# A decoder layer on one core: attention recorded as six streams instead of four, and a group prepared in two pairs of sequences

## The chip, the core and the metric

The kernel runs on one NeuronCore of a Trainium2 chip. The metric is the device time of one execution in microseconds. TensorE is called PE, its weight loads PEld, VectorE is DVE, ScalarE is ACT, GpSimd is POOL, and SyncE, which issues most DMAs, is SP. All data are 32-bit floats.

## What is computed

The reference is one pre-norm decoder layer over 32 sequences of 100 tokens with 256 features, and a context of 361 rows for each sequence:

```python
x = x + self_attention(layernorm(x))            # 16 heads of 16, rotary positions, causal
x = x + cross_attention(layernorm(x), ctx)      # 16 heads of 16, 361 keys, with biases
x = x + soft_moe(layernorm(x))                  # 8 experts of 128 slots

def soft_moe(x):
    xn, sn = rmsnorm(x), rmsnorm(slot_embeds)
    logits = einsum('bnd,esd->bnes', xn, sn)
    dispatch = softmax(logits, axis=1)          # over the 100 tokens
    combine = softmax(logits.reshape(b, n, e * s), axis=-1)   # over the 1024 slots
    slots = einsum('bnd,bnes->besd', xn, dispatch)
    h = gelu(slots @ w1 + b1)                   # 256 -> 1024
    eo = h @ w2 + b2                            # 1024 -> 256
    return einsum('bmd,bnm->bnd', eo, combine)
```

## The kernel before

The 32 sequences form eight groups of four (SIZES), numbered from 0. For each group the eight experts run in turn. Expert weights are loaded once for each group and expert, into single buffers.

PE executes in program order, since each matmul and transpose is recorded with keep_in_program_order. The order is made while the program is recorded, by a small planner: `pe["t"]` is a planned time that each matmul advances by its columns, and each piece of other work is a Python generator (class Steps) that yields the planned time at which it may go on, a demand on the score bank, and a condition. The loop between(), called between the matmuls of an expert, runs those streams that fit at that moment; drive() runs streams until one of them, its goal, is done, without expert matmuls in between. The other engines' order is left to the scheduler.

There are four streams, tried in this order:

- own: self_attention. For sequence b it does layer norm, transposes (`ps_xhT`), q and k with rotation (`ps_qk`), v (`ps_v`), scores (`sc`), softmax over all 16 heads on DVE, POOL and ACT (tile `p`), transposes of the weights (`ps_pT`), the spread of the reciprocal sums over rows (`wide`, `ps_rb`), values (`ps_av`) and the output projection (`ps_o`). It may run up to three sequences ahead of the last one that has crossed.
- scores: cross_softmax. For each of four quads of heads it does four matmuls side by side into four banks (`xsc`), two maxima on DVE (`xnmax`) and four exponentials on ACT (`xp`). Up to NXP = 3 results wait to be turned.
- steps: prepare(g+1). It holds cross_attention of the group's four sequences (turning `xp` with `ps_xpT`, then `ps_xav` and `ps_o`), the norm of each token row (tokens) with its transposes, then the routing logits of all eight experts (`ps_lt`, 400 columns each), their transposes for two sequences at a time (`ps_l`), the softmax over slots, and `ps_nm`, which spreads the negative maxima over all partitions.
- inputs: cross_inputs. For sequence b it turns the context (`ps_cT`), makes keys (`ps_kT`), waits for b's self-attention, makes queries (`ps_xq`), and then makes values (`ps_xv`) once the previous sequence's values are used up:

```python
yield after(0, lambda: b <= state["crossed"] + 2)
cT, kT = yield from context(b)
yield after(0, lambda: b in selfed)
```

route(k, e) makes what expert e needs: the softmax over tokens (`dT`), its transposes (`pd`, `disp`), the slots (`sl`, `slT`), and the combine weights (`cT`). run_expert then does `ph` (256 to 1024, with Gelu on ACT into `hT`), `pe` (1024 to 256), and `py`, which adds the result into the residual tile `x`. Routing of the next expert starts inside the `pe` stage.

PSUM is divided into one tile of four banks for scores (ps_s: `sc`, `xsc` and `ps_l` take turns in it), two banks for small work (ps_m) and two for the experts (ps_b); before the first expert small work may use ps_b too. The logits need `routed >= NE - 1`, that is, the last expert of the previous group must have been routed, because the eight `lt` buffers are then free.

At the start no expert can run: prepare(0) is driven to its end together with the other streams. At the end of each group, halfway through the last expert's `pe` stage, whatever is missing of prepare(g+1) is driven to its end.

## Time and profile before

| what | us |
|---|---|
| median of three runs (lowest, highest) | 3293.3 (3292.8, 3299.66) |
| the profiled execution | 3290.16 |
| its span, first to last instruction | 3288.4 |
| PE busy | 3080.1 |
| ACT busy | 1447.5 |
| DVE busy | 1292.9 |
| POOL busy | 555.5 |
| first `ph` begins | 294.7 |

The page gives busy time for each engine, and for each group of instructions by source line. A wait is listed as the engine that waited, what it was about to do, and what released it. In the views by stage each row holds the stretch, its length, and for each engine its busy time with the number of instructions that began in it, then the granted share of PE's clock, the DMA share and GB/s. A matmul of 32-bit floats is two instructions of PE, so a program matmul counts twice there.

### The profile page before, as it was taken

Reading aid. Unit: us, or ns where it says so; the run is one execution under the profiler, and the core shown is the slowest. Engines: PE = TensorE matmul, PEld = TensorE weight load, DVE = VectorE, ACT = ScalarE, POOL = GpSimd, SP = SyncE. Lnnn points to the kernel's source line nnn. Section 1 sums busy time; section 2 is a strip of 40 time slices with the busy share of each in tenths; the row PEclk is TensorE's granted clock in tenths of the full one; section 3 lists DMA queues with packets and bytes.
Section 4 is the critical chain, followed back from the end, with each engine's and each line's share of the span. In section 5 each row is a group of like instructions: output and inputs, shape, how many; then the busy total and the mean of one; then the engine's idle time right before and its main releaser. Section 6 shows DMA issues by size and latency. Waiting matters only on the chain.

```text
span 3288.4 us, 44719 instructions
## 1 busy us (share of the span) xinstructions
PE 3080.1 (94%) x18481; PEld 2126.4 (65%) x18481; DVE 1292.9 (39%) x2477; ACT 1447.5 (44%) x2824; POOL 555.5 (17%) x816
## 2 busy tenths in 40 slices
PE   5778999999999999999999999999999999999999
PEld 3556666666666666666666666766666666666666
DVE  3554444433443443434443343443443433422211
ACT  2444445344454445444445345444445444534331
POOL 3231211103101121112211011210211102000000
PEclk9788999999999999999999999999999999999999
DMA  3000111111111111112111111112111111111121
GB/s 107 10 10 13 47 49 56 47 51 60 47 45 59 52 45 64 47 43 67 47 45 52 60 45 59 47 45 65 47 45 48 57 48 55 42 63 64 63 64 55
DMA packets 116316, 167.51 MB, mean 51 GB/s; under 512 B 4521, under 2 KB 99729, under 8 KB 116113
## 3 DMA queue, kind: packets, MB, share of 16 engines
q1 hardware_dynamic: 112368, 161.01, 15.1%
q10 hardware_dynamic: 3744, 3.65, 0.4%
q8 instruction: 145, 2.38, 0.3%
q14 instruction: 59, 0.48, 0.0%
HBM read 161.36 MB, written 3.28 MB: 50 GB/s over the span
## 4 chain that ended last, share of the span: by engine, by line
PE 80%; ACT 9%; DVE 5%; POOL 4%; issue 2%; DMA 0%; ACTq 0%; DVEq 0%; POOLq 0%
PE ph L88 24%; PE pe L88 24%; PE sl L88 3%; PE ps_xpT L92 3%; PE xsc L88 3%; PE ps_lt L88 2%; PE ps_xv L88 2%; PE py L88 2%; PE ps_xav L88 2%; PE ps_kT L88 2%; ACT L873 2%; PE ps_o L88 2%; ACT hT L873 2%; POOL p L437 1%; ACT xp L611 1%
## 5 line engine op out<-in xcount | busy, mean ns | idle before, releaser
L88 PE MATMUL pe<-w,hT 128*128 128x256 f32 x4096 | 1048.3, 386 | 1.8 <-ACT hT L873 1.8
L88 PE MATMUL ph<-slT,w 128*128 128x512 f32 x2048 | 994.4, 602 | 25.3 <-ACT hT L873 24.6
L88 PEld LDWEIGHTS pe<-w,hT 128*128 128x128 f32 x4096 | 734.8, 191 | 170.3 <-issue 73.1
L873 ACT ACTIVATE hT<-ph,cols 128x512 f32<-128x512 f32 x512 | 350.3, 687 | 486.7 <-PE ph L88 480.8
L88 PEld LDWEIGHTS ph<-slT,w 128*128 128x128 f32 x2048 | 357.2, 190 | 291.1 <-issue 224.8
L611 ACT ACTIVATE xp<-xsc,xnmax 100x361 f32<-100x361 f32 x512 | 282.9, 558 | 263.6 <-DVE xnmax L607 262.8
L607 DVE TENSOR_REDUCE xnmax<-xsc 100x2 f32<-100x722 f32 x256 | 231.7, 905 | 250.6 <-PE xsc L88 172.8
L92 PEld LDWEIGHTS ps_xpT<-ident,xp 100*128 100x128 f32 (+1 forms) x1536 | 183.7, 157 | 120.9 <-issue 63.3
L629 DVE COPY xpT<-ps_xpT 128x400 f32<-128x400 f32 (+1 forms) x256 | 145.1, 570 | 261.8 <-PE ps_xpT L92 261.2
L830 POOL TENSOR_TENSOR dT<-dT,ri 128x400 f32<-128x400 f32 x64 | 55.3, 864 | 1012.3 <-DVE ri L829 968.5
L92 PE MATMUL ps_xpT<-ident,xp 100*128 100x100 f32 (+1 forms) x1536 | 203.9, 260 | 19.8 <-ACT xp L611 9.6
L873 ACT ACT_TABLE_LOAD x136 | 174.5, 1283 | 83.1 <-PE ph L88 81.3
L890 DVE TENSOR_TENSOR eo<-pe,b 128x512 f32<-128x512 f32 x128 | 88.2, 689 | 279.9 <-PE pe L88 279.3
L823 POOL TENSOR_TENSOR cT<-lt,nmB 128x400 f32<-128x400 f32 x64 | 66.2, 1039 | 679.9 <-ACT nmB L810 354.3
L903 DVE SCALAR_TENSOR_TENSOR x<-py,cinv,x 100x256 f32<-100x256 f32 x256 | 112.1, 479 | 164.5 <-PE py L88 163.6
L88 PEld LDWEIGHTS sl<-disp,xn 100*128 100x128 f32 x1024 | 133.9, 194 | 20.9 <-ACT rb L354 8.0
L88 PE MATMUL sl<-disp,xn 100*128 100x128 f32 x1024 | 137.3, 278 | 9.1 <-ACT rb L354 5.2
L437 POOL TENSOR_TENSOR p<-p,nmax 100x800 f32<-100x800 f32 x64 | 96.1, 1523 | 249.9 <-DVE nmax L436 239.5
L88 PE MATMUL py<-eo,cT 128*100 128x256 f32 x512 | 131.8, 380 | 0.8 <-DVE eo L890 0.8
L88 PE MATMUL xsc<-kT,xqT 32*100 32x361 f32 x1024 | 112.8, 510 | 10.4 <-ACT xp L611 9.5
L848 DVE TENSOR_SCALAR slT<-sl,cols 128x512 f32<-128x512 f32 x128 | 95.5, 746 | 65.0 <-PE sl L88 64.4
L310 POOL TENSOR_SCALAR ve<-bnmv 100x1 f32<-100x1 f32 x96 | 21.4, 223 | 582.7 <-DVE bnmv L308 579.2
(143 smaller groups left out, 3416.6 us busy)
## 6 DMA issues: line engine op xcount, KB each, us to landing
w<-in_L_ffn_w_dram SPq DMA_DIRECT2D x128, 1024.0 KB
ctx<-in_ctx_dram SPq DMA_DIRECT2D x32, 256.0 KB
b<-in_L_ffn_b_dram SPq DMA_DIRECT2D x64, 128.0 KB
ctx<-in_ctx_dram SPq DMA_DIRECT2D x32, 105.0 KB
x<-in_x_dram SPq DMA_DIRECT2D x8, 400.0 KB
out_dram<-x SPq DMA_DIRECT2D x16, 200.0 KB
se<-n_L_ffn_slot_embeds_dram ACTq DMA_DIRECT2D x1, 1024.0 KB
rawWk<-in_L_attn_Wk_dram ACTq DMA_DIRECT2D x1, 256.0 KB
```

The costliest lines, as they stand in the source:

```text
L88: tc.keep_in_program_order(nc.tensor.matmul(out, lhsT=lhsT, rhs=rhs, **kw))
L92: tc.keep_in_program_order(nc.tensor.transpose(out, in_, identity))
L437: nc.gpsimd.tensor_tensor(p[:, hs, :], p[:, hs, :], nmax[:, hs].unsqueeze(2).to_broadcast([S, HPC, S]), ALU.subtract,)
L607: nc.vector.tensor_reduce(nmax[:, c, q : q + 2, r], sc[:S, q : q + 2, :SK], axis=AX.X, op=ALU.max, negate=True,)
L611: nc.scalar.activation(p[:, q, :], sc[:S, q, :SK], AF.Exp, bias=nmax[:, c, q, r : r + 1], accum_out=sums[:, c, q, r : r + 1],)
L629: nc.vector.tensor_copy(pT[:n], ps[:n, : HG * S])
L823: nc.gpsimd.tensor_tensor(cT, k.lt[e], k.nmB, ALU.add)
L830: nc.gpsimd.tensor_tensor(dT, dT, ri.unsqueeze(2).to_broadcast([P, nb, S]), ALU.mult)
L848: nc.vector.tensor_scalar(slT[:, dc, :], sl[:, : nb * NS], cols[:, NGM + dc : NGM + dc + 1], None, ALU.mult)
L873: nc.scalar.activation(h[:, :n], ph_[:, :n], AF.Gelu, bias=cols[:, e * NHC + hc : e * NHC + hc + 1])
L890: nc.vector.tensor_tensor(eo[:, :m], po[:, :m], b2.unsqueeze(1).to_broadcast([P, m, D]), ALU.add)
L903: nc.vector.scalar_tensor_tensor(xg[g][:, b, :], py[:S, i, :], k.ci[:, b : b + 1], xg[g][:, b, :], ALU.mult, ALU.add,)
```

## The change

- cross_inputs becomes two streams: cross_queries, which makes a sequence's queries once its self-attention is done, and cross_context, which makes keys and values. cross_softmax waits for both.
- prepare becomes two streams: crossing, which runs cross_attention and tokens for one sequence after another, and prepare, which takes the finished rows from the list turning. With the two of own and scores this makes six.
- What limits how far a stream runs ahead is no longer the last crossed sequence but the group: near(b, ahead) lets it run to the end of the group in preparation and `ahead` sequences on (one at the start).
- prepare works on two sequences at a time: it turns their rows, makes the logits of two experts in one bank (two experts of 200 columns), copies and reduces both at once, and then transposes and normalizes that pair before it takes the next. The `lt` buffers hold two experts each.
- In cross_scores both maxima come first, then the four exponentials.
- tokens does five POOL instructions instead of eight.
- A planned delay of 1.2 is added after the keys.

```diff
-    ltp = pool("ltp", 8)
+    ltp = pool("ltp", NE // 2)
...
+    def near(b, ahead):
+
+        last = FIRST[state["group"] + 1] + SIZES[state["group"] + 1]
+        return b < last + (ahead if state["group"] >= 0 else 1)
...
-            yield after(0, lambda: b <= state["crossed"] + 3 and WHERE[b][0] in xg)
+            yield after(0, lambda: near(b, 3) and WHERE[b][0] in xg)
...
-            if b + 1 < B and b <= state["crossed"] + 2:
+            if b + 1 < B and near(b + 1, 3):
                 yield from begin(b + 1)
...
+        for q in range(0, NQ, 2):
+            nc.vector.tensor_reduce(
+                nmax[:, c, q : q + 2, r], sc[:S, q : q + 2, :SK], axis=AX.X, op=ALU.max,
+                negate=True,
+            )
         for q in range(NQ):
-            if q % 2 == 0:
-                nc.vector.tensor_reduce(
-                    nmax[:, c, q : q + 2, r], sc[:S, q : q + 2, :SK], axis=AX.X, op=ALU.max,
-                    negate=True,
-                )
             nc.scalar.activation(
                 p[:, q, :], sc[:S, q, :SK], AF.Exp, bias=nmax[:, c, q, r : r + 1],
...
-    def cross_inputs():
+    def cross_queries():
 
         for b in range(B):
-            yield after(0, lambda: b <= state["crossed"] + 2)
-            cT, kT = yield from context(b)
-            yield after(0, lambda: b in selfed)
+            yield after(0, lambda: near(b, 1) and b in selfed and b < 2 + len(queried))
             yield after(1.2)
             steps_ = turned(b)
...
+            queries[b] = cross_q(xhT), after(2.2)[0]
+
+    def cross_context():
+
+        for b in range(B):
+            yield after(0, lambda: near(b, 1))
+            cT, keys[b] = yield from context(b)
             yield after(0, lambda: state["valued"] >= b - 1)
             yield from context_values(cT)
             given.add(b)
...
-        nc.gpsimd.tensor_scalar(q, mv[:, 1:2], float(D), None, ALU.mult)
-        nc.gpsimd.tensor_tensor(q, q, rstd, ALU.mult)
-        nc.gpsimd.tensor_tensor(q, q, rstd, ALU.mult)
-        nc.gpsimd.tensor_scalar(q, q, 1e-24, None, ALU.max)
+        nc.gpsimd.tensor_scalar(q, mv[:, 1:2], float(D), rstd, ALU.mult, ALU.mult)
+        nc.gpsimd.tensor_scalar(q, q, rstd, 1e-24, ALU.mult, ALU.max)
...
+    def crossing():
+
+        for b in range(B):
+            g, i = WHERE[b]
+            yield after(0, lambda: g <= state["group"] + 1)
+            if i == 0:
+                groups[g] = Group(g)
+            yield from cross_attention(b)
+            yield after(0)
+            k = groups[g]
+            tokens(k, i, b)
+            due = after(6.5)[0]
+            turning.append((due, k, i))
+            yield after(0)
...
         for b0 in range(0, nb, 2):
             m = min(2, nb - b0)
-            yield scores_after(turned_, 2.8, 6)
+            for i in range(b0, b0 + m):
+                yield after(0, lambda: len(turning) > 0)
+                due, k, at = turning.pop(0)
+                assert at == i
+                yield max(due, pe["t"]), None, None
+                transposed(k.xn[:, i, :], k.xnT[:, :, i * S : (i + 1) * S])
+            yield after(1.5, lambda: state["slots"].it is None and state["routed"] >= NE - 1)
+            if b0 == 0:
+                k.logits()
+            cols_ = slice(b0 * S, (b0 + m) * S)
+            for e in range(0, NE, 2):
+                ps = bank("ps_lt").rearrange("p (e n) -> p e n", e=2)[:, :, : m * S]
+                for i in range(2):
+                    for dc in range(ND):
+                        matmul(
+                            ps[:, i, :], lhsT=snT[:, dc, (e + i) * NS : (e + i + 1) * NS],
+                            rhs=k.xnT[:, dc, cols_],
+                            start=(dc == 0), stop=(dc == ND - 1),
+                        )
+                nc.scalar.copy(k.lt2[e // 2][:, :, cols_], ps)
+                nc.vector.tensor_reduce(
+                    k.mx[:, e : e + 2, b0 : b0 + m],
+                    ps.rearrange("m e (b n) -> m e b n", b=m), axis=AX.X, op=ALU.max,
+                )
+                yield after(0)
+
+            yield scores_after(after(1.2)[0], 2.8, 6)
             ps = score_banks("ps_l", 6.5).rearrange("n (b h) s -> n b (h s)", b=2)
...
-            state["routed"] = 0
+            state["routed"], state["group"] = 0, min(g, NG - 2)
...
-            for s in (own, scores, steps, inputs):
+            for s in (*streams[:2], steps, *streams[2:]):
```

## The prediction

> **What bounds the kernel now.** I read the page's first two parts, then busy time by stage, then the waits of TensorE alone, then the timeline around the longest of those waits.
>
> ```profile
> span 3288.4 us, 44719 instructions
> PE 3080.1 (94%) x18481; PEld 2126.4 (65%) x18481; DVE 1292.9 (39%) x2477; ACT 1447.5 (44%) x2824; POOL 555.5 (17%) x816
> PE   5778999999999999999999999999999999999999
> PEclk9788999999999999999999999999999999999999
> ```
>
> PE is busy 94% of the span and no other engine half of it. PE's digits fall below 9 only in the first four slices of 82 us, where the clock dips too. So there are two regimes: a start in which no expert matmul is there to cover waits (the first `ph`, in the view of that tile, begins at 294.7), and after it eight groups of expert work, numbered from 0, limited by PE itself. The stages in numbers (PE busy is the second figure, the granted clock stands after POOL):
>
> ```profile
> 74.10:121.90 47.80, 35.10 (x339) 25.36 (x338) 25.01 (x46) 20.52 (x61) 7.63 (x9) 0.77 0.03 9
> 121.90:158.20 36.30, 26.67 (x249) 20.51 (x248) 21.45 (x43) 14.18 (x41) 11.66 (x18) 0.76 0.04 11
> 158.20:197.00 38.80, 27.32 (x309) 20.55 (x308) 23.71 (x47) 18.32 (x55) 13.68 (x21) 0.88 0.04 11
> 250.10:294.70 44.60, 35.61 (x231) 25.53 (x230) 27.24 (x54) 21.39 (x51) 14.60 (x16) 0.81 0.00 1
> 690.40:1086.50 396.10, 380.94 (x2308) 262.13 (x2308) 160.61 (x308) 183.29 (x353) 68.61 (x100) 0.99 0.16 52
> ```
>
> Before 294.7 nothing is full: one sequence costs 36 to 48 us, of which DVE works 21 to 25 and PE 27 to 35 at a clock of 0.76 to 0.88. That is a chain of dependences. From 294.7 a group takes 396.1 us and PE is idle 15 of them. PE's waits over the span:
>
> ```profile
> PE ph L88 <- ACT hT L873: 24.6, 21, 1.7
> PE ps_l L92 <- ACT ps_l L795: 23.1, 7, 3.6
> PE ps_rb L92 <- DVE wide L344: 13.9, 3, 6.5
> PE ps_xq L88 <- ACT xhT L330: 11.8, 3, 5.3
> PE sc L88 <- ACT xp L611: 6.5, 2, 3.8
> ```
>
> The last three lie wholly in the start. `ps_l` is the pair-of-sequences transposes at the end of each group; in the groups it is the largest single wait.
>
> **The start, step by step.** The single four-bank tile for scores sets the cadence. The timeline gives the first `xsc` at 74.1 and then 85.8, 99.5, 109.5 (sequence 0), 115.1, 121.9, 128.1, 134.1 (1), 158.2, 164.6, 170.6, 177.5 (2), 197.0, 204.2, 211.1, 216.8 (3), 229.0, 238.9, 256.3 (4). Undisturbed, they follow each other at 5.6 to 7.2, mean 6.3. But from 134.1 to 158.2 and from 177.5 to 197.0 there are holes of 24.1 and 19.5. The reason is in the code: cross_inputs(2) may start only when sequence 0 has crossed (its `ps_o` is at 122.7), and then goes through context, turned, cross_q in a row; and a self-attention `sc` sits in each hole. In the changed program's PE order queries are a stream of their own: `ps_xq` of sequences 2, 3 and 4 stands well before the `xsc` that need them, and `xsc` of sequence 1's last quad is followed by sequence 2's first with only 12 transposes between.
>
> One turn of the bank in the old kernel:
>
> ```profile
> 128.14 0.87 PE L88 MATMUL xsc<-kT,xqT 32*100 32x361 f32 x8
> 129.07 0.91 DVE L607 TENSOR_REDUCE xnmax<-xsc 100x2 f32<-100x722 f32 x1 [0.62 <-PE xsc L88]
> 130.81 0.56 ACT L611 ACTIVATE xp<-xsc,xnmax 100x361 f32<-100x361 f32 x1
> 131.50 0.91 DVE L607 TENSOR_REDUCE xnmax<-xsc 100x2 f32<-100x722 f32 x1 [0.56 <-ACT xp L611]
> 132.44 0.56 ACT L611 ACTIVATE xp<-xsc,xnmax 100x361 f32<-100x361 f32 x1 [0.98 <-DVE xnmax L607]
> 134.10 0.87 PE L88 MATMUL xsc<-kT,xqT 32*100 32x361 f32 x8
> ```
>
> The second maximum waits for the first two exponentials. After the change both maxima go first and the first exponential waits for both (in the new order only it carries a wait). The sum on paper barely moves: 0.93 to the first maximum, 2 x 0.91, 4 x 0.54 (one exponential's pitch, 130.27 to 130.81), about 0.4 to the next matmul, 5.3 against 5.96 here, of which some 0.3 are queueing. A maximum that blocks DVE's queue is gone, but the first two exponentials come 0.9 later; behind that wait on ScalarE stand copies and, in the groups, Gelu, which the old order held up twice per quad, so I charge it nothing. I take 6.0 for 6.3.
>
> New start: the instructions ahead of the first `xsc` grow by six `ps_xv`, a context's six `ps_cT` and four `ps_kT`, some 6 us of PE work, mostly in the holes of 33 to 74; I put its start at 76. Until the first `ps_l` the new order has 19 `xsc` and, behind the first, three `sc`. A `sc` holds the bank some 3.1 (82.7 to 85.8). 19 x 6.0 + 3 x 3.1 = 123, so 199 if the bank never rests. It will: the self-attention of sequences 1 to 4 is now packed early, and `ps_rb` will again wait for a `wide` behind a self-softmax on DVE (6.5 twice in the old start), and `ps_xq` for ACT (5.3). I charge 15 of the 41 us that `ps_rb`, `ps_xq`, `xsc` and `sc` wait in the old start: first `ps_l` at 214. DVE is no bound there: it works 21 to 25 per sequence, and (214 - 76) / 4.75 sequences leaves 29.
>
> Tail: the second pair's logits are 16 matmuls of 200 columns, 5.4 us; then `ps_l`, 1.8, the maximum, 2.3, `ps_nm`, `pd`, `sl`. The old start needs 12.4 from its second `ps_l` (282.3) to `ph`; with 10 in front for the first `ps_l`, two turns and the logits this is 22. First `ph` at 236, against 294.7: 58 less.
>
> But the old start did more ahead. By the PE order up to the first `ph`, it holds 7 self-attentions (56 `sc`), 6 contexts and 6 `xq`; the new one 5, 5 and 5. That work comes back where PE is full. In steady rows a self-attention is 16 `ps_qk` 1.8, `ps_v` 0.86, `sc` 0.7, `ps_pT` 1.4, `ps_rb`, `ps_av`, `ps_o` 1.9, `ps_xhT` 0.3: 7.0; a context 3.2, a query 1.2. 2 x 7.0 + 3.2 + 1.2 = 18 returned. **Start: -58 + 18 = -40.**
>
> **The groups.** Logits: 16 matmuls of 400 columns become 32 of 200 per group, and the weight loads double. A load lasts 193 ns in its row; were it exposed, 64 instructions would cost 12.4 against 32 x 0.336 = 10.8, +1.6 a group. But the old `sl`, 128 columns with the same loads, runs 16 in 2.05 us, so loads overlap down to 0.112 each; 200 columns at half of 0.336 are 0.168. I take nothing; the upper end is +13 in all.
>
> Group ends. The old stall:
>
> ```profile
> 1066.15 1.28 ACT L795 ACT_TABLE_LOAD   x1
> 1067.44 1.09 ACT L795 ACTIVATE ps_l<-ps_l,cnm 100x1024 f32<-100x1024 f32 x1
> 1068.70 3.56 PE L92 MATMUL ps_l<-ident,lt 128*100 128x128 f32 x16 [3.56 <-ACT ps_l L795]
> ```
>
> The second `ps_l` follows the first by 9 matmuls and waits 3.56 for its exponentials, at each of six ends (23.1 less 1.7 in the start; the seventh is already spread). In the new order, at the ends of groups 1 to 5, the first pair's `ps_l` lies far ahead and `ps_nm` keeps seven to ten program matmuls of cover (4.3 us, against 2.29 + 0.45 on DVE). At the end of group 0 it is worse: `ps_xhT`, 16 `ps_lt`, one `xsc`, `ps_l`, `ps_nm` follow with no expert matmul between, since the forced drive runs there. I price that as 1 for the copy of `xhT`, 2 for logit banks behind a softmax, 1 for the score bank, 3.3 for the maximum and diag: 7.5. Sum: -6 x 3.56 + 7.5 = **-14**.
>
> **ScalarE's tables, and a rule that speaks against the change.**
>
> ```profile
> L873 ACT ACT_TABLE_LOAD x136 | 174.5, 1283 | 83.1 <-PE ph L88 81.3
> L611 ACT ACT_TABLE_LOAD x61 | 78.3, 1283 | 9.0 <-DVE xnmax L607 8.3
> ```
>
> All such rows sum to 271 loads. In the new ScalarE order Gelu and Exp alternate 294 times, 22 more than the 272 of the old order. The Trainium skill ("ScalarE: Activation LUTs", What ACT_TABLE_LOAD costs) puts a switch at about 2.66 us, 1283 ns of load and 1380 ns of drain. By it the change adds 59 us to ScalarE and, if that reached PE, would eat the whole gain. The rows show the 1283; how much arrives at PE is another matter: `ph` waits 24.6 us for `hT` in all, for 271 loads 0.09 each. 22 x 0.09 = 2. I take +2, ScalarE having 54% idle in a group, and keep 59 as the far end of a rival.
>
> **Costed at nothing:** three fewer GpSimd instructions per sequence (96, near 0.2 us each): POOL is 17% busy, so only the latency to `xn` shrinks, by about 1.3 us, once at the end of the start and inside my 22; in the groups expert matmuls cover it. The added 1.2 us in context is planner's delay, no instruction. DMA issues keep their number; context loads go ahead of need and PE waits for none after 10 us.
>
> Sum: -40 - 14 + 2 = -52, so a profiled span of 3236. The profiled execution took 3290.2, 3.1 under the median of 3293.3; applied to the median, **3241**.
>
> **Rivals.**
> 1. *The start shrinks half as much* (in-order queues: packed self-softmaxes hold `wide` and `xhT` back, the clock stays near 0.8): the first `ph` at 265, -30 + 18 - 14 + 2 = -24, 3269. For it: DVE's and ACT's share of those waits. Against: the holes of 24 and 19 have a cause that is removed. 0.22. A harmless reshuffle that returns everything is its far end.
> 2. *Slower.* Attention now runs in bursts bounded by groups (near), ends early in groups 1, 3, 5, and makes ScalarE switch tables inside Gelu runs, so `ph` waits for `hT`. The old waits besides `ps_l` are about 12 a group; the gain is gone once they grow by 52 / 7 = 7.4 a group. With the page's whole 59 exposed: 3300. Against: ACT is busy 46% in a group. 0.08.
> 3. *Better:* the bank reaches its paper cadence of 5.4 and the groups lose a third of their other waits: 19 x 0.6 + 15 + 7 x 4 = 54 more at most; I put the case at 30 more, 3211. 0.12.
> The main case has 0.58.
>
> **Numbers.** About 0.2% (7 us) can be told from no change here. Range 3206 to 3280: the main case with its uncertain terms (stalls of the start +-15, groups +-15), most of 1 and 3, without 2. Faster 0.88, same 0.05 (far end of 1), slower 0.07.
>
> **What would show it.** First `ph` near 236; `xsc` from the second sequence on at about 6 us without holes; groups 1 to 5 near 392.5 where it was 396.1, and group 0 near 414 (two self-attentions returned, 14, and 4 for its end); `ps_l` <- ACT near nothing; 22 or so more table loads. The forecast is wrong if the first `ph` stays over 270, or if `ph` <- `hT` passes 60 us.

## The result, and the profile after

| kernel | median, us (lowest, highest) | ratio to before, 95% interval |
|---|---|---|
| before | 3293.3 (3290.4, 3299.7) | 1 |
| after | 3286.07 (3279.91, 3288.43) | 0.9971 (0.9959, 0.9983) |

The change gains 7 us by the medians; by the interval of the ratio it is 0.17 to 0.41%, 6 to 14 us. The forecast was 3241 with a range from 3206 to 3280: the sign is right, the size is not. The profiled execution of after took 3288.43, the top of its runs, so its span is only 1.7 us under that of before; the medians say how much was gained, the traces say where. From the page of after:

```profile
span 3286.7 us, 45298 instructions
PE 3087.9 (94%) x18737; PEld 2158.8 (66%) x18737; DVE 1271.9 (39%) x2477; ACT 1464.3 (45%) x2846; POOL 547.1 (17%) x720
PE   5779999999999999999899999999899999999999
PEclk9789999999999999999999999999999999999999
```

The main waits of PE over the span (us in total, times, longest). A row `ps_qk` <- `xhT` of 34.0 stands above them, 22.9 of it in one wait at the very start (21.8 before):

```profile
PE ph L88 <- ACT hT L899: 28.8, 28, 1.7
PE ps_pT L92 <- ACT kT L564: 22.0, 4, 7.2
PE xsc L88 <- ACT xp L617: 21.0, 17, 3.0
PE pe L88 <- ACT hT L899: 14.9, 12, 2.2
PE ps_rb L92 <- DVE wide L344: 9.1, 2, 4.6
```

PE's busy digits climb a slice earlier than before, and the row `ps_l` <- `ps_l` of 23.1 us is gone. In its place stands a row that the old trace has not: `ps_pT` waits 7.2 us at a time for a copy on ACT. Note the last column, the longest single wait: a figure of 7 among figures of 1 to 5 is one event worth looking up. The stages of after, cut at each group's first `ph` (PE busy second, granted clock after POOL):

```profile
0.00:265.00 265.00, 187.40 (x1551) 142.76 (x1552) 137.14 (x280) 104.06 (x300) 76.90 (x112) 0.84 0.13 38
265.00:692.70 427.70, 402.56 (x2520) 278.73 (x2518) 172.47 (x333) 194.21 (x377) 80.72 (x100) 0.98 0.14 44
692.70:1088.60 395.90, 379.74 (x2340) 264.94 (x2340) 158.36 (x309) 184.33 (x355) 68.39 (x89) 0.99 0.16 51
1088.60:1482.60 394.00, 379.56 (x2339) 263.88 (x2337) 157.96 (x306) 189.33 (x359) 67.46 (x87) 1.00 0.16 52
2670.90:3020.10 349.20, 343.98 (x2004) 240.42 (x2003) 124.87 (x241) 156.61 (x290) 39.02 (x56) 1.00 0.17 54
```

Beside the same cuts of before, and the forecast's sum put on the same places:

| stage | before | after | forecast for it | measured |
|---|---|---|---|---|
| start, to the first `ph` | 294.7 | 265.0 | -58 | -29.7 |
| group 0 | 397.0 | 427.7 | +17 | +30.7 |
| groups 1 to 5 together | 1980.1 | 1978.2 | -18 | -1.9 |
| groups 6 and 7 | 616.6 | 615.8 | with tables and the returned context: +6 | -0.8 |

So the start gave half of what was expected, group 0 took all of that back, and the groups gave nothing. Four questions follow.

### The profile page after: what moved, and what is told of

It is laid out like the page before. It is cut to its first block, busy times and chain, and to the rows that moved or that the text cites. A ratio compares the mean times of both kernels' runs of the same rounds, so it can differ in the third digit from the quotient of the medians.

```text
span 3286.7 us, 45298 instructions
## 1 busy us (share of the span) xinstructions
PE 3087.9 (94%) x18737; PEld 2158.8 (66%) x18737; DVE 1271.9 (39%) x2477; ACT 1464.3 (45%) x2846; POOL 547.1 (17%) x720
## 4 chain that ended last, share of the span: by engine, by line
PE 78%; ACT 10%; DVE 5%; POOL 4%; issue 2%; DMA 0%; ACTq 0%; DVEq 0%; POOLq 0%
PE pe L88 24%; PE ph L88 22%; PE sl L88 3%; PE ps_xpT L92 3%; PE py L88 3%; ACT xp L617 3%; PE xsc L88 3%; PE ps_xv L88 2%; PE ps_xav L88 2%; ACT L899 2%; PE ps_lt L88 2%; DVE xnmax L612 2%; PE ps_o L88 2%; PE ps_qk L88 2%; ACT hT L899 2%
## 5 line engine op out<-in xcount | busy, mean ns | idle before, releaser
L88 PE MATMUL pe<-w,hT 128*128 128x256 f32 x4096 | 1047.6, 388 | 15.3 <-ACT hT L899 14.9
L88 PE MATMUL ph<-slT,w 128*128 128x512 f32 x2048 | 1003.8, 604 | 29.1 <-ACT hT L899 28.8
L617 ACT ACTIVATE xp<-xsc,xnmax 100x361 f32<-100x361 f32 x512 | 280.9, 563 | 116.5 <-DVE xnmax L612 80.6
L612 DVE TENSOR_REDUCE xnmax<-xsc 100x2 f32<-100x722 f32 x256 | 220.8, 899 | 166.2 <-PE xsc L88 165.4
L92 PEld LDWEIGHTS ps_xpT<-ident,xp 100*128 100x128 f32 (+1 forms) x1536 | 175.6, 153 | 114.2 <-issue 75.5
L92 PE MATMUL ps_xpT<-ident,xp 100*128 100x100 f32 (+1 forms) x1536 | 192.0, 254 | 9.2 <-ACT xpT L633 5.8
L88 PEld LDWEIGHTS sl<-disp,xn 100*128 100x128 f32 x1024 | 134.5, 194 | 14.9 <-DVE x L929 4.2
L88 PE MATMUL xsc<-kT,xqT 32*100 32x361 f32 x1024 | 112.7, 510 | 22.8 <-ACT xp L617 21.0
```

Source lines behind the costliest of these rows:

```text
L88: tc.keep_in_program_order(nc.tensor.matmul(out, lhsT=lhsT, rhs=rhs, **kw))
L92: tc.keep_in_program_order(nc.tensor.transpose(out, in_, identity))
L612: nc.vector.tensor_reduce(nmax[:, c, q : q + 2, r], sc[:S, q : q + 2, :SK], axis=AX.X, op=ALU.max, negate=True,)
L617: nc.scalar.activation(p[:, q, :], sc[:S, q, :SK], AF.Exp, bias=nmax[:, c, q, r : r + 1], accum_out=sums[:, c, q, r : r + 1],)
```

## The experiments

All times are medians, and all ratios are to the kernel before as it ran beside each experiment. Its median was between 3293.3 and 3300.3 us, so a difference in us between two kernels that did not run side by side is good to some 7 us; the ratios are safer. Edits of the changed kernel are named as such; those of the kernel before, too.

**The groups: what took the place of the `ps_l` wait.** The timeline of POOL, ACT and PE in group 1 of after, around the wait of 7.2 us:

```profile
769.06 1.25 POOL L752 TENSOR_SCALAR xn<-x,bnmv,r 100x256 f32<-100x256 f32 x1
770.93 1.23 POOL L318 TENSOR_SCALAR xh<-x,bnmv,rstd 100x256 f32<-100x256 f32 x1
772.25 0.72 POOL L664 TENSOR_TENSOR x<-x,boB 100x256 f32<-100x256 f32 x1
774.39 1.24 POOL L318 TENSOR_SCALAR xh<-x,bnmv,rstd 100x256 f32<-100x256 f32 x1
775.59 1.02 POOL L394 TENSOR_TENSOR ropeu<-ropeu,rope 128x400 f32<-128x400 f32 x1
776.70 1.02 POOL L395 TENSOR_TENSOR ropet<-ropet,ropeu 128x400 f32<-128x400 f32 x1
...
777.75 0.81 ACT L398 ACTIVATE rotk<-ropet,half 128x200 f32<-128x200 f32 x2 [10.38 <-POOL ropet L395]
778.47 0.54 ACT L564 ACTIVATE kT<-ps_kT,cols 128x361 f32<-128x361 f32 x1
778.92 0.48 ACT L460 COPY pT<-ps_pT 100x400 f32<-100x400 f32 x1
...
779.07 0.91 PE L92 MATMUL ps_pT<-ident,p 100*100 100x100 f32 x4 [7.20 <-ACT kT L564]
```

Read it from below. PE waits for a bank that a copy of `kT` on ACT must empty; that copy is short, but stands in ACT's queue behind `rotk`, and `rotk` waits 10.4 us for POOL. DVE had delivered its part of the rotation at 769.7 (`STREAM_SHUFFLE`, 769.10 for 0.61 us), but POOL took it up only at 775.59: from 766.09 on, sixteen POOL instructions without a gap stood ahead: the token norm of one sequence, the query norm of another and further norms. They belong to three streams now and come due together. The first experiment lets the rotation past that queue, by giving its two POOL instructions to DVE; PE's order stays the same.

`e1_rope_dve`, in rotation() of the changed kernel:
```diff
-        nc.gpsimd.tensor_tensor(by(u), by(u), table(1), ALU.mult)
-        nc.gpsimd.tensor_tensor(t, t, u, ALU.add)
+        nc.vector.tensor_tensor(by(u), by(u), table(1), ALU.mult)
+        nc.vector.tensor_tensor(t, t, u, ALU.add)
```


> The changed kernel with the two POOL instructions of the rotation (1.02 us each, tiles ropeu and ropet) done by DVE instead; PE's order is the same. Theory P (POOL's queue): in the changed kernel several streams hand POOL their norms at once, the rotation stands behind them, ScalarE stands in order before rotk (10.4 us at 767 to 778), the copy of kT behind it holds a bank, and PE's ps_pT waits 7.2. Then rotk's waits on POOL, 111 us in the groups, fall below 30, the 7.2 waits of groups 1, 3 and 5 and the 3.2 of group 0 go, and each such group loses 5 to 9 us: 20 to 30 in all, near 3260. Rival R (waits only move: another queue holds PE at the same places): under 6 us, 3281 to 3287, with a new longest wait of PE of the same size.

Measured: 3248.46 us (3242.81 to 3252.2), ratio 0.9842 (0.9823, 0.9862), 38 us under the changed kernel (42 by the ratios), more than the 20 to 30 of its theory. ACT's waits of `rotk` fall from 119.1 us to 15.5. Groups 1, 3 and 5 take 385.3 to 387.0 us instead of some 396; groups 2 and 4 stay at 394. The start is 262.8, group 0 420.6. The largest waits of PE in group 1 of this kernel:

```profile
PE ph L88 <- ACT hT L899: 3.2, 3, 1.3
PE xsc L88 <- ACT xp L617: 2.4, 2, 2.2
```

and in group 2:

```profile
PE ps_rb L92 <- DVE wide L344: 4.6, 1, 4.6
PE ph L88 <- ACT hT L899: 3.5, 4, 1.3
```

The 7.2 is gone. But group 1 is 10 us shorter, more than that wait. Its row in the view by stage, to be read beside the one of after above:

```profile
683.30:1068.70 385.40, 376.95 (x2340) 263.69 (x2340) 162.63 (x317) 184.58 (x355) 60.42 (x81) 1.00 0.16 53
```

PE is idle for 8 us where it was 16, and its busy time for the same matmuls is 2.8 us less, at a granted clock of 1.00 for 0.99. Over the span, of the 40 us between the two traces 27 are idle time of PE and 13 busy time. In the even groups another in-order stop remains: `wide`, a copy of 0.3 us, stands in DVE's queue behind the sums of a self-attention, which wait for ACT and POOL.

`e6_rope_dve_before` makes the same edit in the kernel before:

> The kernel before with the two POOL instructions of the rotation done by DVE. In the changed kernel this won about 38 us. Theory P in full (the change itself made POOL's queue a convoy, by letting tokens, queries and the next self-attention ask for their norms at once): here there is little to win, under 12 us, since PE's longest waits are others (ps_l 3.6, ps_kT 2.5). Rival: the rotation on POOL is too late in any order; 20 us or more.

Measured: 3286.84 us (3284.15 to 3287.99), ratio 0.9966 (0.9955, 0.9977). By the ratio's interval it gains 8 to 15 us there, and some 40 in the changed kernel. So most of what the queue costs is made by the change. ACT waited for the rotation before, too, but not as long at a time; the first line is from before, the second from after:

```profile
ACT rotk L398 <- POOL ropet L395: 75.7, 31, 6.8
ACT rotk L398 <- POOL ropet L395: 119.1, 30, 10.4
```

`e9_old_chain` puts the longer POOL chain back into the changed kernel:
```diff
-        nc.gpsimd.tensor_scalar(q, mv[:, 1:2], float(D), rstd, ALU.mult, ALU.mult)
-        nc.gpsimd.tensor_scalar(q, q, rstd, 1e-24, ALU.mult, ALU.max)
+        nc.gpsimd.tensor_scalar(q, mv[:, 1:2], float(D), None, ALU.mult)
+        nc.gpsimd.tensor_tensor(q, q, rstd, ALU.mult)
+        nc.gpsimd.tensor_tensor(q, q, rstd, ALU.mult)
+        nc.gpsimd.tensor_scalar(q, q, 1e-24, None, ALU.max)
...
-        nc.gpsimd.tensor_scalar(r, r, float(D) ** 0.5, rstd, ALU.mult, ALU.mult)
+        nc.gpsimd.tensor_scalar(r, r, float(D) ** 0.5, None, ALU.mult)
+        nc.gpsimd.tensor_tensor(r, r, rstd, ALU.mult)
```


> The changed kernel with the eight GpSimd instructions that prepare one sequence's tokens put back in place of the five; nothing else. Theory (GpSimd's queue is full at the odd groups' hole, so each instruction put back ahead of the rotation delays it): three instructions of about 0.3 to 0.4 us put back hold the rotation about 1 us longer in groups 1, 3 and 5 and less elsewhere; groups 1, 3 and 5 some 0.5 to 1.5 us longer each, 2 to 8 us in all, 3288 to 3294 us. Rival (the chain is only one of several items ahead of the rotation, and the shorter one was hidden): nothing, within 2 us of 3286, and the wait of PE for ps_pT in group 1 stays at 7.2 us.

Measured: 3291.63 us (3287.29 to 3294.24), ratio 0.9984 (0.9978, 0.9991). Against the changed kernel's 0.9971 that is 0.13% or some 4 us, but the intervals touch. In the trace group 0 is 1.6 us longer and groups 1 and 2 are 1.1 and 1.4, of which only 0.2 and 0.4 are idle time of PE; groups 3 to 5 stay within 0.4, and the wait in group 1 is 7.4 for 7.2. The size is in the theory's span, but its place, 1 us on the rotation, is not what the trace shows. By the two intervals the shorter chain is worth between nothing and about 9 us.

`e7_dve_subtracts_too` adds to e1 the self-softmax's subtraction, from POOL to DVE (line 437, gpsimd to vector):

> The changed kernel with the rotation on DVE and also the subtraction of the row maxima in the self-softmax (tile p, 2 x 1.52 us on POOL for each sequence) on DVE. Theory Q (a self-softmax closes DVE's in-order queue while it waits for POOL's 3 us and ScalarE's exponentials; that is what makes an interval of xsc that holds an sc last 10 to 23 us in the start, and what makes ps_rb wait 4.6 for wide in groups 2 and 4): first ph from 263 to 250 or less, the 4.6 falls below 2, total 3220 to 3238. Rival: DVE, with 63 us more work, only fills up; first ph 258 or later, total within 6 of 3248.

Measured: 3264.53 us (3262.87 to 3267.83), ratio 0.9905 (0.9887, 0.9923), 16 us slower than e1, outside both expectations. The wait for `wide` grows to 5.8 us and stays, and the first `ph`, at 261.3 for 262.8, does not come to the 250 of the theory. Shortening the chain by filling the queue in which the waiting copy stands does not help. So the next experiment takes the copy out of that queue.

`e12_rope_dve_wide_pool` is e1 with the cross attention's `wide` made by POOL:
```diff
-    def widened(rinv):
+    def widened(rinv, engine=nc.vector):
...
-        nc.vector.tensor_copy(wide, rinv.unsqueeze(2).to_broadcast([S, heads, DK]))
+        engine.tensor_copy(wide, rinv.unsqueeze(2).to_broadcast([S, heads, DK]))
...
-                wide = widened(rinv)
+                wide = widened(rinv, nc.gpsimd)
```


> The changed kernel with the rotation's two instructions on VectorE (3248.5 us) and, with it, the copy that widens the cross attention's reciprocals moved from VectorE to GpSimd. Theory (in groups 2 and 4 PE waits 4.6 us for this copy, which stands in VectorE's queue behind the sums of a self attention): the wait goes, groups 2 and 4 come to 387 to 391 us from 394, 3238 to 3245 us. Rival (GpSimd, slow at a copy with a broadcast operand, gives the copy late, or the queue behind it moves the stop to another bank): 3248 to 3262 us.

Measured: 3238.77 us (3234.93 to 3240.8), ratio 0.9823 (0.9806, 0.984), the fastest of all kernels here. Its interval overlaps that of e1; what tells the two apart is groups 2 and 4, 391.0 us against 394.2 and 394.4, and their wait:

```profile
PE ps_rb L92 <- POOL wide L344: 2.0, 1, 2.0
```

**The order of maxima and exponentials.** The forecast had charged it nearly nothing. `e2_max_old_order` restores the old order in the changed kernel, with PE's order the same:
```diff
-        for q in range(0, NQ, 2):
-            nc.vector.tensor_reduce(... negate=True)
         for q in range(NQ):
+            if q % 2 == 0:
+                nc.vector.tensor_reduce(... negate=True)
             nc.scalar.activation(...)
```


> The changed kernel with the old order in cross_scores (maximum, two exponentials, maximum, two exponentials); PE's order is the same. Theory X (the block of four exponentials that waits for both maxima holds Gelu up): PE's waits of ph and pe for hT, 43.7 us in the changed kernel against 26.4 before, come back to about 28, and the time falls by 10 to 16, near 3273. Rival: the old second maximum blocks DVE again, and the start's cadence of xsc goes from 6.1 to 6.4, first ph 5 to 8 later and the whole 5 to 10 slower, near 3293. Neither: 3283 to 3289.

Measured: 3343.05 us (3342.35 to 3346.05), ratio 1.0132 (1.0115, 1.0149): 57 us slower than with the new order (53 by the ratios), which neither expectation had. Start +1.7, group 0 +10.3, groups 1 to 5 +5 to +11 each, group 6 +5.6. From its waits:

```profile
PE xsc L88 <- ACT xp L617: 48.8, 26, 3.5
...
ACT xp L617 <- DVE xnmax L613: 201.6, 148, 7.3
DVE xnmax L613 <- ACT xp L617: 132.6, 93, 3.1
```

In the changed kernel the first is 21.0, the second 80.6 and 56.7 more at a table load behind it, and there is no row of the third kind: twice per quad the old order makes ACT wait for DVE and DVE for ACT, and each waits with all that is queued behind it. PE waits 28 us more for the score banks. Group 1 shows where the rest lies:

```profile
704.70:1111.50 406.80, 384.04 (x2339) 267.91 (x2339) 160.14 (x309) 188.25 (x357) 69.16 (x89) 0.98 0.15 50
```

Beside the changed kernel's row, PE is idle 22.8 us for 16.2, and busy 4.3 longer with the same matmuls, at a clock of 0.98 for 0.99. Over the span of the two traces it is 42 us more of idle time, the 28 among them, and 15 more of busy time.

`e5_max_alone` makes the same edit alone, in the kernel before:

> The kernel before with only the new order in cross_scores (both maxima, then four exponentials); PE's order is the same as before. Taken out of the changed kernel that order cost 57 us. Theory S (it is a gain of its own, and the streams, the limits and the pairs together lose what it wins): 30 to 60 faster than before, 3240 to 3265, each group near 388. Rival I (it only pays in the changed kernel, where another stream's work stood behind the second maximum): within 10 of 3295.

Measured: 3292.62 us (3285.13 to 3300.82), ratio 0.9986 (0.9977, 0.9995). 0.05 to 0.23%, 2 to 8 us, where the same edit is worth 57 us under six streams. `e11_max_rope_before` has this edit and the rotation on DVE in the kernel before:

> The kernel before with both maxima ahead of the exponentials and the rotation's two GpSimd instructions on VectorE; four streams, old logits and old chain. If the two edits add up: 3293.3 - 0.7 - 6.4, about 3286 us, and groups of about 395 us. That would leave about 38 us of the changed kernel with the rotation on VectorE (3248.5 us) to the six streams and the pairs. Rival (the streams give nothing that these two edits would not give by themselves): 3245 to 3260 us.

Measured: 3290.08 us (3283.27 to 3293.21), ratio 0.9977 (0.9968, 0.9985), no more than the rotation alone. Between this kernel and e1 stand the six streams with their limits, the pairs and the shorter chain: 3290.1 - 3248.5 = 41.6 us. They show only when the rotation does not queue. That this is near the 52 of the forecast is chance. Between the two traces (36 us apart) the start is 31 shorter and group 0 is 26 longer, 5 gained together where the forecast had 41; groups 1 to 5 gain 35 where it had 18.

**The streams and the pairs, each without the other.** `e4_split_alone` gives the kernel before the streams cross_queries and cross_context in place of cross_inputs, and nothing else:
```diff
-    def cross_inputs():
+    def cross_queries():
         for b in range(B):
-            yield after(0, lambda: b <= state["crossed"] + 2)
-            cT, kT = yield from context(b)
-            yield after(0, lambda: b in selfed)
+            yield after(
+                0, lambda: b <= state["crossed"] + 2 and b in selfed and b < 2 + len(queried)
+            )
...
+    def cross_context():
+        for b in range(B):
+            yield after(0, lambda: b <= state["crossed"] + 2)
+            cT, keys[b] = yield from context(b)
```


> The kernel before with one part of the change: queries and context as two streams, with the old limits by the last crossed sequence and the old prepare. If the two holes of 24.1 and 19.5 between sequences in the start came from the single stream, as the prediction says: first ph from 294.7 to 270 or less, total near 3268. Rival (the limits by the crossed sequence, or the self-attention in the hole, keep them): first ph 285 or later, total within 8 of 3293.

Measured: 3318.18 us (3316.28 to 3323.31), ratio 1.0057 (1.0039, 1.0076). Slower (groups 1 to 5 by 4 to 6 us each, which is not explained here); and the start stays at 295.1, with holes between `xsc` at 135.3 and 153.3 and at 174.4 and 189.3. Before the first of them the query is ready (`ps_xq` at 134.3; in the kernel before it came inside the hole, at 151.4), and the hole is still 18.0 long, with a self-attention's `sc` in it. In the second the query is late as it was (`ps_xq` at 185.1), behind the `ps_qk` and `ps_v` of a self-attention. So the single stream of cross inputs is at most a part of the cause of the holes. The other part of what the forecast named, the limit by the last crossed sequence, still stands in e4; the changed kernel has neither, and what its start looks like is told below.

`e10_no_pairs` keeps the six streams and takes the pairs out of the changed kernel: prepare turns all tokens of the group, then makes the logits of one expert per bank, 400 columns, then both `ps_l`.
```diff
-        for b0 in range(0, nb, 2):
-            ...
-            for e in range(0, NE, 2):
-                ps = bank("ps_lt").rearrange("p (e n) -> p e n", e=2)[:, :, : m * S]
+        for i in range(nb):
+            ...
+            transposed(k.xn[:, i, :], k.xnT[:, :, i * S : (i + 1) * S])
+        for e in range(NE):
+            ps = bank("ps_lt")
...
+        for b0 in range(0, nb, 2):
+            m = min(2, nb - b0)
+            yield scores_after(turned_, 2.8, 6)
```


> The changed kernel, with its six streams, but the logits as before: of a whole group at a time, after the group's last sequence, one expert in a bank, and both exponentials' banks one after the other. Theory (the pairs are what removed the 3.56 us wait for ps_l at a group's end): that wait is back in each of groups 0 to 5, about 3 to 3.6 us a group, 18 to 22 us in all, 3304 to 3308 us. Rival (the wait that went was replaced by others of the same length, and pairs also add their own stops in the middle of a group): 0 to 8 us slower or even a little faster, 3280 to 3294 us.

Measured: 3341.01 us (3338.28 to 3344.21), ratio 1.0134 (1.0114, 1.0155), 55 us slower than with pairs, more than either expectation. Its waits in group 1:

```profile
PE ps_pT L92 <- ACT kT L564: 7.2, 1, 7.2
PE ps_l L92 <- ACT ps_l L820: 4.3, 1, 4.3
```

The wait for `ps_l` is back with 4.3, as the theory had it. But the rest is larger: the start is 274.2 (+9.2), group 0 +6.1, and groups 1 to 5 are all alike at 402.2 to 403.0 us, each with the 7.2 that with pairs only every second group has. Of the 55 us the returned `ps_l` waits are 26 (31.4 over the span, less 5.0 in the start). As in e2, part of the time is PE's busy time: of 53 us between the traces 38 are idle time and 15 busy time. Six streams and their limits without pairs are 46 us slower than the kernel before (44 by the ratio), even with the new order of the maxima; the pairs pay for that. The limits alone, and the split of crossing from prepare alone, were not run.

**The start and group 0.** Does the start shrink because the streams feed it better, or because there is less in it? `e3_start_runs_ahead` gives the start of the changed kernel the same lead as the groups, so that it does seven self-attentions as the old start did, with five contexts and queries where that had six:
```diff
-        return b < last + (ahead if state["group"] >= 0 else 1)
+        return b < last + ahead
```


> The changed kernel in which near() gives the streams their full lead in the start too, so that the start holds seven self-attentions as before the change (it had five). Theory H (work in the start is nearly free, and group 0, 30.7 us longer than before, pays for what was handed back): first ph moves from 265 to no more than 272, group 0 falls from 427.7 to 405 or less, the whole is 13 to 18 shorter, near 3270. Rival: the start is bound by the same queues, the two self-attentions cost there what they cost in group 0 (first ph 279 or later), and the whole stays within 5 of 3286.

Measured: 3299.62 us (3296.85 to 3302.97), ratio 1.0005 (0.9995, 1.0014). The first two stages:

```profile
0.00:303.90 303.90, 211.18 (x1735) 161.72 (x1736) 153.68 (x312) 113.99 (x322) 92.24 (x129) 0.81 0.11 33
303.90:700.00 396.10, 380.28 (x2337) 265.19 (x2336) 156.24 (x302) 184.11 (x355) 66.04 (x84) 0.98 0.14 47
```

With a context and a query less than the old one, this start takes 303.9 us under six streams, 9 more than under four. So it was emptied, not shortened: the two self-attentions cost 38.9 us in the start and 31.6 in group 0, 16 to 20 each, where the forecast returned 7.0 each. The whole is 13 us slower than the changed kernel.

Their place in the start, from DVE's timeline. The `xsc` at 116.5 gets its first maximum at 122.28:

```profile
114.49 1.89 DVE L430 TENSOR_TENSOR p<-sc,causal 100x800 f32<-100x800 f32 x2 [0.66 <-PE sc L88]
116.29 1.87 DVE L436 TENSOR_REDUCE nmax<-p 100x8 f32<-100x800 f32 x2
118.08 1.05 DVE L635 COPY xpT<-ps_xpT 128x400 f32<-128x400 f32 x2
119.90 0.99 DVE L442 TENSOR_REDUCE sums<-p 100x8 f32<-100x800 f32 x1 [0.77 <-ACT p L441]
121.38 0.99 DVE L442 TENSOR_REDUCE sums<-p 100x8 f32<-100x800 f32 x1 [0.49 <-ACT p L441]
122.28 0.90 DVE L612 TENSOR_REDUCE xnmax<-xsc 100x2 f32<-100x722 f32 x1
```

The four banks hold scores that are done, for nearly 5 us, while DVE finishes a self-softmax that itself waits for POOL and ACT. The `sc` had left its banks early, as the forecast said; it is its softmax that stands in the way of the next one. ACT adds to it: the second maximum is done at 124.1, but the exponentials start at 127.82, behind copies of `pT` in ACT's queue, of which the first waited 4.5 us for PE's transposes.

The longest step between two `xsc`, 130.2 to 152.9, is another matter. PE's timeline, some lines left out:

```profile
130.16 1.54 PE L88 MATMUL xsc<-kT,xqT 32*100 32x361 f32 x8 [1.94 <-ACT xp L617]
...
139.06 2.23 PE L88 MATMUL ps_xav<-xpT,vpad 128*32 128x100 f32 x48
...
143.34 0.94 PE L88 MATMUL sc<-rotk,ropet 32*100 32x200 f32 x16
...
148.40 4.54 PE L88 MATMUL ps_xv<-xwWv,ctxT 128*128 128x256 f32 x12 [2.03 <-DVE x L365]
152.88 0.87 PE L88 MATMUL xsc<-kT,xqT 32*100 32x361 f32 x8
```

The exponentials are done at 137.6 and the `sc` has left the banks at 146.2, when DVE has read it. So the banks stand empty from 137.6 to 143.3 and from 146.2 to 152.9, some 12 us, while PE goes through other pieces in its recorded order (2.0 of it waiting for DVE). This step lies between the first two quads of sequence 1, whose query had been ready since 105.3: neither a late query nor a held bank makes it.

So the start has other holes, not fewer. At the places of the old ones, between sequences 1 and 2 and between 2 and 3, the `xsc` now follow each other at 5.0 and 5.3. But steps of 14.2, 13.6 and 22.7 stand ahead of that, where the self-attentions are now: the last quad of sequence 1 comes at 165.8, where it came at 134.1 before, and the first of sequence 3 at 200.7 for 197.0.

Is it the clock, granted at 0.70 in the stretch from 80.9 to 152.9? `e8_dummies_in_start` fills PE in the start with three matmuls that nothing uses, ahead of each `ps_qk`:
```diff
+        if state["group"] < 0 and "xWk" in wT:
+            for _ in range(3):
+                tc.keep_in_program_order(nc.tensor.matmul(
+                    ps, lhsT=ident, rhs=wT["Wk"].rearrange("p c d -> p (c d)"),
+                    start=True, stop=True,
+                ))
```


> The changed kernel with three extra matmuls of 512 columns (2.6 us of PE at full clock) ahead of ps_qk of sequences 1 to 4 in the start; they write the bank that ps_qk then overwrites, and fill PE's 3.9 us waits for xhT. Theory C (between 81 and 153 PE is busy 57 of 72 us at a granted clock of 0.70, so the clock, not the queues, makes the start long): the granted clock there rises to 0.85 or more, and first ph comes before 258 although PE has some 10 us more work. Rival: queues set the pace; first ph at 263 to 275, with whatever clock.

Measured: 3287.28 us (3281.02 to 3289.41), ratio 0.9971 (0.9961, 0.9981). The same stretch in the changed kernel:

```profile
80.90:152.90 72.00, 56.70 (x481) 43.05 (x480) 41.57 (x79) 27.43 (x76) 20.96 (x23) 0.70 0.00 1
```

and with the added matmuls:

```profile
80.90:152.90 72.00, 58.42 (x458) 42.14 (x459) 41.71 (x82) 26.52 (x74) 21.91 (x25) 0.75 0.00 1
```

The start stays at 263.8 against 265.0, though PE has thirty instructions more in it (17.1 us in their row) and is busy 194.4 us for 187.4. So the waits that these fill were free. But the clock rises only to 0.75, where the theory asked for 0.85 or more: what a faster clock would do to the start this run does not show, and it stays open.

Another question was whether 16 to 20 us is the price of a self-attention anywhere, or of many in one stage. `e13_lead_of_one` hands them on evenly, to group 6:
```diff
-            yield after(0, lambda: near(b, 3) and WHERE[b][0] in xg)
+            yield after(0, lambda: near(b, 1) and WHERE[b][0] in xg)
...
-            if b + 1 < B and near(b + 1, 3):
+            if b + 1 < B and near(b + 1, 1):
```


> The changed kernel with self attentions allowed to run one sequence past the next group, not three, in the groups as well as in the start. The start keeps its five; group 0 does four and no longer six; groups 1 to 5 four each, as before; group 6 does three and no longer one. Theory (piling: six in one stage is what makes them dear, and where there is room one costs its matmul work, some 6.5 to 7 us): group 0 goes from 427.7 to 396, group 6 from 349.2 to 362 to 365, the sum 15 to 19 us less, 3267 to 3271 us. Rival (a self attention costs some 16 us wherever it runs): group 6 grows by 31 and the time stays at 3284 to 3289 us.

Measured: 3288.15 us (3287.74 to 3292.41), ratio 0.9968 (0.9955, 0.998), no different from the changed kernel. Group 0 falls by 30.5 to 397.2; group 6 rises by 22.5 to 371.7, between the theory's 13 to 16 and the rival's 31, and groups 1 to 5 rise by 2 to 3 us each: every one of them now has the `wide` wait, of 5.6 us, and none the 7.2. The sum is what the rival said, but only partly by its reason. Of the 30.5 in group 0, 20.4 are PE's busy time and 10.1 idle time; of the 22.5 in group 6, 17.0 and 5.6.

`e14_start_of_four` holds the start to group 0's own four sequences:
```diff
-        return b < last + (ahead if state["group"] >= 0 else 1)
+        return b < last + (ahead if state["group"] >= 0 else 0)
```


> The changed kernel with the start held to the four sequences of group 0 and nothing beyond them: one self attention, one context and three cross score steps less in the start, which go to group 0. By the price seen in the start (19.5 us a self attention, 6.1 us a score step) the start comes to 230 to 246 us. Theory (piling): group 0, with seven self attentions, grows by as much or more, 20 to 40 us, and the time is 3280 to 3300 us. Rival (work in the start, at a granted clock of 0.75, is dearer than anywhere else): group 0 grows by 12 to 20 us and the time falls to 3265 to 3278 us.

Measured: 3304.42 us (3297.05 to 3309.13), ratio 1.0012 (1.0005, 1.0018). The start falls by 24.5 to 240.5 and group 0 rises by 41 to 468.8. Group 0's last expert alone takes 108.8 us where it took 64.7, and the granted clock of the group falls from 0.98 to 0.95: the start has only moved into the drive at the group's end, where no expert matmuls cover it. Here the theory of piling holds.

`e15_best_with_lead_of_one` joins the lead of one to e12:

> The lead of one sequence together with the rotation on VectorE and the cross attention's widening copy on GpSimd (3238.8 us). Theory (piling): group 0 from 420.4 to 387 to 391, group 6 from 348.6 to 362 to 365, 3219 to 3226 us. Rival (a self attention costs the same everywhere): 3236 to 3242 us.

Measured: 3255.85 us (3251.73 to 3257.51), ratio 0.9868 (0.9852, 0.9884), 17 us slower than e12, outside both expectations. Group 0 gains 31 and the start 7; group 6 loses 21 and groups 1 to 5 lose 4 to 8 us each, 29 in all. In e12 groups 1, 3 and 5 have no large wait; with a lead of one all five wait 3.1 for `wide`, and 4.3 for `hT` at `pe` in place of 1.9 to 2.2.

## Why the prediction failed, and where it held

Its sum was -58 in the start, +18 returned, -14 at the group ends, +2 for tables. The terms, with what they measured:

- **"The holes of 24 and 19 have a cause that is removed": moved, not removed.** This is the step that failed first. In the changed kernel the two holes are gone from their places, but the time is not: a step of 22.7 and two of 14 stand earlier, beside the self-attentions, and through sequence 3 the new start is behind the old. Its gain comes after that, where the old start has two more self-attentions (`sc` at 235.4 and 268.0). e4 took away the single stream alone, one hole stayed with the query ready, and the start kept its length; e3 gave the new program the old self-attentions, and the start was 9 longer than the old one. The old trace had told it: its four steps with an `sc` in them took 11.7, 24.1, 19.5 and 9.9, on average 10 more than the 6.3 of the others. The first `ph` at 265 is rival 1's figure, but not for all of its reasons: in the start PE has no large wait for `wide` any more (the row's 9.1 us lie in groups 2 and 4).
- **"A `sc` holds the bank some 3.1": the mis-sized term.** The holding was right, but what PE, DVE and ACT do around a self-attention delays the scores by more. In the trace after there are 19 `xsc` from 80.9 to 239.2. Without a `sc` between, they follow each other at 6.6 (13 steps from 152.9 to 239.2 in 86.3), where the forecast took 6.0. The five steps before, from 80.9 to 152.9, take 72.0 with three `sc`: (72.0 - 5 x 6.6) / 3 = 13 each. This 13 is a remainder shared out, not the length of any one wait: in one step DVE and ACT hold the banks, in the longest PE's own order leaves them empty, and no run took these apart. So from the first `xsc` to the first `ps_l` it is 19 x 6.6 + 3 x 13 = 164 (measured 163.4) against 19 x 6.0 + 3 x 3.1 + 15 = 138. With 5 for the later first `xsc` (80.9 for 76) and 1 less in the tail (20.7 for 22) that is the 29 by which the start was missed.
- **"18 returned": 30.7.** Group 0's growth is 22 us of PE's busy time and 8.5 of waits more than before. e13 shows that the price depends on the place: 15 a piece in group 0, where it is 10 of busy time and 5 of idle time, and 11 in group 6, where it is 8.5 and 2.8. So the 7.0 of PE work was not far off in group 6, but in no stage was a self-attention had for that alone.
- **"-6 x 3.56": the waits went, the time did not.** The `ps_l` waits are gone, and e10 shows 4.3 a group if they return. But a group's waits sum to 15.9 and 14.2 us by turns, as before (14.9): the 7.2 on the rotation in odd groups and the 4.6 on `wide` in even ones came in. The forecast had reckoned POOL as 17% busy and the shorter chain at nothing; the share of the span did not show that sixteen POOL instructions in a row would stand ahead of the rotation in one place. e1 removes it and gains 38. The term also left out that PE's busy time for the same matmuls moves with its waits (13 of the 40 us in e1).
- **"The order barely moves the sum": right for the kernel before, wrong for the changed one.** 0.05 to 0.23% alone, 2 to 8 us (e5), 57 in the changed kernel (e2). It was summed over one turn of the bank, not over the two queues. So the sign came right by luck: without the term that the forecast put at next to nothing, the change would have cost 1.3%.
- **Tables.** The forecast counted 294 loads for 272, and the rows of the two traces sum to just that (its 271 for the old rows is one short). The largest of after:

```profile
L899 ACT ACT_TABLE_LOAD x147 | 188.6, 1283 | 78.5 <-PE ph L88 76.2
```

  PE's waits for `hT` grew from 26.4 (24.6 at `ph`, 1.8 at `pe`) to 43.7 (28.8 and 14.9), 17 us where the forecast had 2. An estimate from the Trainium skill's 2.66 us a switch ("ScalarE: Activation LUTs", What ACT_TABLE_LOAD costs) would have put 59 us on ACT. The traces show less: where ACT does not wait, an instruction starts 1.31 us after the end of the one before the load (median in before and in after), so 22 loads are some 29 us of ACT by this measure. No run here changed the tables alone, so how much of the 17 they cause is open. The two did not go together in other runs: e4 has 14 loads fewer than before and 7 us more of these waits (33.5), and e2 has 14 more than after and no more of them (43.7).
- **Held:** the tail, the vanished wait, the count of loads, and `ph` <- `hT` far below 60.

In sum, three terms failed: the start, of which half came; the price of the work handed back; and the groups, where the removed wait was replaced by waits in the queues of POOL and DVE. With the queue of the rotation taken out on both sides the rest of the change is worth 41.6 us (e11 against e1), a gain that an in-order queue on an engine that is 17% busy had hidden. It is not the forecast's gain: it comes from groups 1 to 5, not from the start.

## What to carry to other kernels

When streams are made independent, work that used to come one after the other comes due together. Look at each engine's queue at the places where it bunches, however low its share of the span: what is urgent there (here the rotation, and a copy of 0.3 us) waits behind what is not, and everything in order behind it on the next engine waits too. Price a moved step by what it costs in the stage that takes it, with the queues as they are there, and do not add the values of edits measured apart: the order of the maxima was worth at most 8 us in one program and 57 in another.

## What had not been expected of the hardware

- The DVE form of the rotation's add takes 0.57 us where POOL's takes 1.03 (128 x 400, mean of its row in e1 and in before). Two such instructions a sequence are cheap on the busier engine and dear on the idle one when it stands in a chain.
- Filling waits in the start with matmuls raised the granted clock only from 0.70 to 0.75 over 72 us, and moved the time by nothing.
- The same PE program ran 57 us apart when only the order of instructions on DVE and ACT was different (after against e2).
- PE's busy time for the same matmuls moves with the granted clock, also where its waits are the same. Groups 1 and 3 of e11 have 14.4 us of idle PE each:

```profile
688.80:1082.10 393.30, 378.89 (x2307) 259.76 (x2306) 163.19 (x316) 182.30 (x353) 60.62 (x92) 1.00 0.16 52
1477.00:1876.00 399.00, 384.56 (x2307) 263.34 (x2306) 163.26 (x316) 182.31 (x353) 60.64 (x92) 0.98 0.16 51
```

  So a difference of a few us between two groups says little until the idle time is put beside it. What sets the clock in a group was not tested.
